# Grouped-query attention in a fused two-layer block: queries of two heads from seven of eight quarter products, with TensorE's order written out

## The chip, the cores and the metric

The kernel runs on one core of a Trainium2 chip. A core has a matrix engine (TensorE, "PE" in the profile, its weight loads "PEld"), a vector engine (VectorE, DVE), an activation engine (ScalarE, ACT), a general engine (GpSimd, POOL) and a synchronising engine (SyncE, SP). Each engine works off its own list of instructions in order; they meet through semaphores. Most DMAs are issued on SP's queue, those of the attention weights' turn on POOL's. The metric is the time of one execution on the device in microseconds (us); a kernel's time is the median of several runs.

## The reference

The whole computation is two blocks on x of shape 4 x 512 x 512 (batch rows b, 512 tokens, 512 channels): a gate, a Mamba-2 layer, a gate, a mixture of experts; then a gate, attention, a gate, an FFN. The change lies in the second block's attention, whose input x is already multiplied by its gate:

```python
b, sq, _ = x.shape                      # 4, 512, 512
q = jnp.einsum('bsh,he->bse', x, w_q).reshape(b, sq, GROUPS, HPG, KVC)   # 4 groups of 4 heads, 128
kv = jnp.einsum('bsh,he->bse', x, w_kv)
k, v = jnp.split(kv, 2, axis=-1)        # one key and one value head for each group
scores = jnp.einsum('bqgpd,bkgd->bgqpk', q, k) * (SCALE / LAYER_INDEX)
scores = jnp.where(causal[None, None, :, None, :], scores, -jnp.inf)
probs = jax.nn.softmax(scores, axis=-1)
ctx = jnp.einsum('bgqpk,bkgd->bqgpd', probs, v).reshape(b, sq, HEADS * KVC)
return jnp.einsum('bse,eh->bsh', ctx, w_dense)
```

All numbers are float32.

## The kernel before

Activations are kept transposed: a tile h of 128 x 4 x 512 holds, for one row b, 512 channels (four blocks k of 128 partitions) by 512 tokens. Attention runs over 64 heads in the order group g, row b, head i of the group; below, head n is 16g + 4b + i. The kernel is written with a framework that orders the instructions of each engine when the kernel is built, by their dependencies and the order of writing; `after(engine)` binds what is written inside it behind the last instruction written so far on that engine. The order is then fixed: a built program has one list for each engine.

Of a head's work there is:

- **queries** (L1648): four matmuls of 512 columns into pq, a PSUM tile of the tag "tp" (two buffers), and ACT's scaling into qT.
- **keys and values** (`start_group`, L1622), once for a group and row: four matmuls of 512 into pk, sixteen of 128 into pv, PSUM tag "mm" (four buffers), and two ACT copies.
- **scores** (L1663): for each of four blocks qi of 128 queries a matmul of (qi+1) x 128 columns into psc (tag "mm"); DVE adds the causal mask (L1677) and takes the negated maximum (L1679); ACT takes the exponential with its sum; DVE takes the reciprocal (L1685), scales (L1686) and turns 32 x 32 blocks (L1690) into `turned`, a tile with two copies. POOL then writes these to DRAM with four DMAs (L1698), and one more (`collect`, L1716) reads them back as pT, the transposed weights. Within `scores`, `nudge` lets one step of the gates of the coming layer be written on DVE and ACT (the lines 259 to 333).
- **context** (L1718): four matmuls of pT and v into pctx, PSUM tag "acc" (two buffers), and ACT's copy into cx, one of five buffers of the pool sm. It runs three heads behind the scores (`held`, `settle`). The last two heads are transposed by TensorE in place of the DMAs (ptp, L1729).
- **dense** (L1753), when a row's four contexts are there: sixteen matmuls of 512 into pd (tag "acc"), in four parts of four, after each of which DVE adds the part to the residual xr (L1765).

In the first group the same engines also combine the experts' results (pcb, L1521) and apply the gates that make h of rows 1 to 3 (`gated`, DVE L406). The pool gp has four buffers of the tag "h"; before, they hold the four rows' h through attention. A group's query weights (1 MB) and key and value weights come in one step ahead by `load_group` (L1487) into the pool wa, with two buffers.

The FFN after attention puts its weights ffg, ffu and ffd over the space of pools that attention used: the pool of the gates, cb (buffers rr of the experts' results), and wa. A load waits until whatever lay there is no longer read. The loads (L1886 to L1889) stand in a row on SP's queue.

Of the kernel before, what the change touches and what calls it, by code (L numbers as in the profile page):

```python
# [10 lines left out]
F32 = mybir.dt.float32  # L11
# [3 lines left out]
ALU = mybir.AluOpType  # L15
# [68 lines left out]
def block_kernel(ctx: ExitStack, tc: tile.TileContext, a: dict, out: bass.AP):  # L84
# [58 lines left out]
    def ps_mm(name):  # L143
        return ps.tile([P, 512], F32, tag="mm", name=name, bufs=4)
# [268 lines left out]
    def gated(l, b, xb, pool, part=slice(0, T), **kw):  # L413
        have((l, b))
        n = part.stop - part.start
        g = pool.tile([P, NC, n], F32, **kw)
        nc.sync.dma_start(out=g, in_=gts[l][b][:, :, part])
        apply_gate(g, xb[:, :, part])
        return g
# [1067 lines left out]
    def load_group(g):  # L1487

        wq = wa.tile([P, NC, HPG * KVC], F32, tag="wq", name="wq")
        w = HPG * KVC  # L1490
        nc.sync.dma_start(
            out=wq, in_=a["w_q"][:, g * w : (g + 1) * w].rearrange("(k p) m -> p k m", p=P)
        )
        wkv = wa.tile([P, 2, NC, KVC], F32, tag="wkv", name="wkv")
        for i in range(2):
            c0 = i * GROUPS * KVC + g * KVC
            nc.sync.dma_start(
                out=wkv[:, i], in_=a["w_kv"][:, c0 : c0 + KVC].rearrange("(k p) m -> p k m", p=P)
            )
        return wq, wkv  # L1500

# [37 lines left out]
    with tc.tile_pool(name="moe_w2", bufs=1, reuse_waits="tile") as wm:  # L1539
# [33 lines left out]
        n = len(nc.cur_bb.bb.instructions)  # L1573
        early_h = gated(2, 0, x[0], wa, tag="wq", name="h2_0")
        early_th = [
# [13 lines left out]
    with att as ph:  # L1589
# [25 lines left out]

        hs = [gp.tile([P, NC, T], F32, tag="h", name="h2")] + [None] * (B - 1)
        nc.sync.dma_start(out=hs[0], in_=early_h)

        class Group:
            pass  # L1620

        def start_group(g, b, w):  # L1622
            u = Group()
            u.g, u.b, u.ctxT = g, b, []
            u.last_row = g == GROUPS - 1 and b == B - 1
            u.wq, wkv = w
            u.h = h = early_h if (g, b) == (0, 0) else hs[b]
            pk = ps_mm("pk")
            for k in range(NC):
                nc.tensor.matmul(  # L1630
                    pk, lhsT=wkv[:, 0, k, :], rhs=h[:, k, :], start=(k == 0), stop=(k == NC - 1)
                )
            u.kT = sm.tile([P, T], F32, tag="kT", name="kT")
            nc.scalar.copy(u.kT, pk)
            pv = ps_mm("pv")
            for t in range(NT):
                for k in range(NC):
                    nc.tensor.matmul(  # L1638
                        pv[:, t * P : (t + 1) * P],
                        lhsT=h[:, k, t * P : (t + 1) * P],  # L1640
                        rhs=wkv[:, 1, k, :],
                        start=(k == 0),
                        stop=(k == NC - 1),
                    )
            u.v = sm.tile([P, NT, KVC], F32, tag="v", name="v")
            nc.scalar.copy(u.v.rearrange("p t d -> p (t d)"), pv)
            return u

        def queries(u, i):
            pq = ps_tp("pq")  # L1650
            for k in range(NC):
                nc.tensor.matmul(  # L1652
                    pq,
                    lhsT=u.wq[:, k, i * KVC : (i + 1) * KVC],
                    rhs=u.h[:, k, :],
                    start=(k == 0),
                    stop=(k == NC - 1),
                )
            qT = sm.tile([P, T], F32, tag="qT", name="qT")
            nc.scalar.mul(qT, pq, SCALE)  # L1660
            return qT

        def scores(u, i, qT):  # L1663
# [5 lines left out]
            for qi in range(NT):  # L1669
                n = (qi + 1) * P  # L1670
                if qi == 0:
                    collect(1)
                psc = ps_mm("psc")
                nc.tensor.matmul(  # L1674
                    psc[:, :n], lhsT=qT[:, qi * P : n], rhs=u.kT[:, :n], start=True, stop=True
                )
                nc.vector.tensor_tensor(psc[:, qi * P : n], psc[:, qi * P : n], mask, ALU.add)  # L1677
# [43 lines left out]
        def context(u, prs):  # L1721
# [18 lines left out]
            pctx = ps_acc("pctx")  # L1740
            for kj in range(NT):
                nc.tensor.matmul(  # L1742
                    pctx[:, kj * P :].rearrange("p (q r j) -> p q r j", r=QUAD, j=SQ),
                    lhsT=u.v[:, kj, :],
                    rhs=pT[:, :, 4 * kj : 10 + kj : 3, :].rearrange("p r q j -> p q r j"),
                    start=(kj == 0),
                    stop=(kj == NT - 1),
                )
            cx = sm.tile([P, T], F32, tag="cx", name="cx", bufs=5)
            nc.scalar.copy(cx, pctx)  # L1750
            u.ctxT.append(cx)

        def dense(u):  # L1753
            for m in range(NC):
                po = ps_acc("pd")
                for i in range(HPG):
                    nc.tensor.matmul(  # L1757
                        po,
                        lhsT=dense_w[u.g][:, i, m * P : (m + 1) * P],
                        rhs=u.ctxT[i],  # L1760
                        start=(i == 0),
                        stop=(i == HPG - 1),
                    )
                xs = x[u.b][:, m, :]
                nc.vector.tensor_tensor(xs, xs, po, ALU.add)  # L1765

        def settle():

            old, done = held.pop(0)
            context(old, done)
            if len(old.ctxT) == HPG:
                dense(old)

# [3 lines left out]
        def begin(n):  # L1779
            g, b, i = heads_[n]  # L1780
            if i == 0:
                if b == 0 and g + 1 < GROUPS:
                    weights[g + 1] = load_group(g + 1)
                groups[g, b] = start_group(g, b, weights[g])
            return groups[g, b], queries(groups[g, b], i)

# [8 lines left out]
        look_ahead(1, (0, 1))  # L1795
        groups = {}
        numbers = iter(range(GROUPS * B * HPG))
        ready, held = begin(0), []
        for n, (g, b, i) in enumerate(heads_):
# [8 lines left out]
            if g == 2 and i == 0 and b < 3:  # L1808
                to, name = ((ffg_d, "gateT"), (ffu_d, "upT"), (ffd_d, "downT"))[b]
                nc.sync.dma_start(out=to, in_=a[name])  # L1810
            if g and b == 0 and i == 3:
                dense_w[g] = load_dense(g)
            if n + 1 < len(heads_):
                ready = begin(n + 1)
            if g == 0 and i == 2 and b + 1 < B:
                act.use(act.EXP)
                hs[b + 1] = gated(2, b + 1, x[b + 1], gp, tag="h", name=f"h2_{b + 1}")
                act.use(act.LOG_EXP)
            prs = scores(u, i, qT)
            held.append((u, prs))  # L1820
            if len(held) > 3:
                settle()
            if n == len(heads_) - 2:
                last_row_over = [
                    i for i in nc.cur_bb.bb.instructions if i.engine == nc.scalar.engine
                ][-1]
        while held:
            settle()
        for _ in making:
            pass  # L1830
# [212 lines left out]
```

## Time and profile before

| | |
|---|---|
| median of three runs | 2239.01 us (2236.49 to 2239.73) |
| the profiled execution | 2242.7 us, span 2241.0 us, mean granted clock of TensorE 0.981 |
| attention, first group | 1120 to about 1334 us of the span |
| attention, second to fourth group | about 1334 to 1995 us |
| FFN | from 1973 (first matmuls, between attention's last) to the end |
| queries, TensorE busy (L1652) | 237.4 us, 512 records of 128x512 |
| dense, TensorE busy (L1757) | 222.4 us, 512 records of 128x512 |
| DVE waiting for dense (L1765) | 196.8 us |
| turned blocks: four DMAs a head (L1698), issue to landing | 208 KB each, 3.8 us |
| pT: one DMA a head (L1716), issue to landing | 832 KB, 7.3 us |

How to read the profile: a group of instructions is named by engine, line, output and input tile and shape; "busy" is the time in which the engine ran them. A matmul of float32 appears as two records. The durations of matmul records overlap and are modelled, so the true price of a row of matmuls is taken from the chain of waits, in which each piece begins where the one before ended. A window row gives, for a stretch of the span, its length and the busy time (and count) of PE, PEld, DVE, ACT and POOL, then the clock granted to TensorE (1.00 is full), the DMA engines' busy share, and GB/s. In the timeline a line is start, duration, engine, line, operation, output and input, shape, count, and in brackets how long the engine had been idle and what ended that.

### The profile page before, as it was taken

How to read it: one execution, taken by the hardware profiler on the slowest of the kernel's cores; microseconds unless marked ns; L12 is line 12 of the kernel's file. 1: busy time of each engine (PE TensorE's matmuls, PEld its weight loads, DVE VectorE, ACT ScalarE, POOL GpSimd, SP SyncE). 2: the span in 40 equal slices, each digit the busy share in tenths (PEclk: the TensorE clock that was granted, in tenths of full speed). 3: DMA queues.
4: the chain of work that ended last, by engine and by line, in shares of the span. 5: the costliest groups of instructions: out<-in, count | busy, mean ns of one | idle time of the engine just before them, and what ended most of it. 6: DMA issues, size and time to landing. Idle time of an engine off the chain costs nothing.

```text
span 2241.0 us, 23830 instructions
## 1 busy us (share of the span) xinstructions
PE 2135.2 (95%) x7570; PEld 1224.9 (55%) x7570; DVE 1526.2 (68%) x3039; ACT 968.9 (43%) x1899; POOL 455.8 (20%) x620
## 2 busy tenths in 40 slices
PE   4979999999999999999998999999999999999998
PEld 2545565565665444444454455555555555568887
DVE  8799889989653566676477766677767765555332
ACT  4576776765732234333254333333334432333221
POOL 4023242422222111222211111112112122100000
PEclk9989999999999999999989999999999999999999
DMA  7542341432424458988676555555645464531100
GB/s 257 195 132 73 107 155 67 156 122 67 167 83 141 152 190 285 382 289 285 211 252 195 179 183 150 160 164 181 185 140 175 141 195 140 185 122 38 38 20 20
DMA packets 112452, 357.38 MB, mean 159 GB/s; under 512 B 14592, under 2 KB 23168, under 8 KB 102912
## 3 DMA queue, kind: packets, MB, share of 16 engines
q1 hardware_dynamic: 78656, 224.43, 29.0%
q0 software_dynamic: 31360, 127.16, 18.9%
q10 hardware_dynamic: 2304, 4.20, 0.5%
q8 instruction: 62, 1.02, 0.2%
q14 instruction: 70, 0.57, 0.1%
HBM read 337.91 MB, written 108.00 MB: 199 GB/s over the span
## 4 chain that ended last, share of the span: by engine, by line
PE 40%; DVE 8%; ACT 1%; DMA 1%; issue 0%; DVEq 0%; ACTq 0%
PE pd L1757 10%; PE pq L1652 6%; PE pctx L1742 4%; PE psc L1674 4%; PE pk L1630 3%; PE pv L1638 3%; PE pfo L1873 2%; PE pfo L1872 2%; PE pfg L1872 2%; PE pfg L1873 2%; PE pfu L1872 2%; PE pfu L1873 2%; DVE nmax L1679 1%; DVE turned L1690 1%; DVE pr L1686 1%; DVE psc L1677 1%
## 5 line engine op out<-in xcount | busy, mean ns | idle before, releaser
L1698 POOL DMA_DIRECT2D turned<-turned x248 | 136.0, 555 | 622.8 <-DVE turned L1690 387.9
L128 ACT ACTIVATE pr<-psc,nmax 128x128 f32<-128x128 f32 (+3 forms) x256 | 134.7, 527 | 286.9 <-DVE nmax L1679 284.2
L1652 PE MATMUL pq<-h,wq 128*128 128x512 f32 x512 | 237.4, 599 | 1.8 <-DVE h L406 1.2
L1757 PE MATMUL pd<-cx,wd 128*128 128x512 f32 x512 | 222.4, 592 | 0.0
L1765 DVE TENSOR_TENSOR xr<-xr,pd 128x512 f32<-128x512 f32 x64 | 44.0, 687 | 196.8 <-PE pd L1757 196.8
L1674 PE MATMUL psc<-kT,qT 128*128 128x128 f32 (+3 forms) x512 | 160.0, 442 | 15.5 <-ACT pr L128 14.4
L1757 PEld LDWEIGHTS pd<-cx,wd 128*128 128x128 f32 x512 | 96.1, 190 | 114.8 <-issue 110.3
L1057 PE MATMUL pc<-h,wxb 128*128 128x512 f32 x320 | 145.6, 610 | 6.6 <-DVE h L406 4.0
L1652 PEld LDWEIGHTS pq<-h,wq 128*128 128x128 f32 x512 | 94.7, 193 | 102.2 <-issue 90.8
L1742 PE MATMUL pctx<-pT,v 128*128 128x512 f32 (+3 forms) x512 | 148.4, 433 | 0.0
L1742 PEld LDWEIGHTS pctx<-pT,v 128*128 128x128 f32 x512 | 96.7, 190 | 76.2 <-issue 50.5
L847 PE MATMUL po<-w,yT 128*128 128x512 f32 x296 | 134.2, 593 | 0.6 <-DMA w<-in_w2x 0.4
L814 PE MATMUL pg<-w,hT 128*128 128x512 f32 x296 | 134.2, 594 | 0.0
L825 PE MATMUL pn<-w,hT 128*128 128x512 f32 x296 | 133.4, 593 | 0.7 <-DMA w<-in_w1x 0.7
L1674 PEld LDWEIGHTS psc<-kT,qT 128*128 128x128 f32 x512 | 84.9, 191 | 74.2 <-ACT pr L128 29.7
L1679 DVE TENSOR_REDUCE nmax<-psc 128x1 f32<-128x128 f32 (+3 forms) x256 | 122.1, 481 | 2.1
L1690 DVE STREAM_TRANSPOSE turned<-pr 128x128 f32<-128x128 f32 x248 | 117.0, 493 | 1.2
L1128 PE MATMUL pz<-wzt,h 128*128 128x512 f32 x256 | 116.6, 605 | 0.3 <-ACT st L1229 0.3
L1276 PE MATMUL po<-wot,yT 128*128 128x512 f32 x256 | 115.4, 605 | 0.0
L1057 PEld LDWEIGHTS pc<-h,wxb 128*128 128x128 f32 x320 | 60.8, 195 | 78.0 <-issue 71.5
L1686 DVE TENSOR_SCALAR pr<-pr,rsum 128x128 f32<-128x128 f32 (+3 forms) x256 | 95.7, 375 | 2.2
L1677 DVE TENSOR_TENSOR psc<-psc,mask 128x128 f32<-128x128 f32 x256 | 70.9, 284 | 37.4 <-PE psc L1674 37.0
(348 smaller groups left out, 4186.3 us busy)
## 6 DMA issues: line engine op xcount, KB each, us to landing
w<-in_w1x SPq DMA_DIRECT2D x76, 1024.0 KB
turned<-turned POOLq DMA_DIRECT2D x248, 208.0 KB, 3.8
pT<-turned POOLq DMA_DIRECT2D x62, 832.0 KB, 7.3
w<-in_w2x SPq DMA_DIRECT2D x38, 1024.0 KB
wb<-in_b1x SPq DMA_DIRECT2D x38, 512.0 KB
lm<-cs SPq DMA_DIRECT2D x32, 512.0 KB
kt<-in_fT SPq DMA_DIRECT2D x62, 256.0 KB
ek<-ek SPq DMA_DIRECT2D x62, 256.0 KB
```

The lines of the kernel that those rows point to most:

```text
L128: nc.scalar.activation(*args, **kw)
L814: nc.tensor.matmul(pg, lhsT=hT[:, k, :], rhs=self.w1[s][0][:, k, :], start=(k == 0), stop=(k == NC - 1))
L1057: nc.tensor.matmul(pc, lhsT=wxb[:, k, m * P : (m + 1) * P], rhs=h[:, k, :], start=(k == 0), stop=(k == NC - 1),)
L1652: nc.tensor.matmul(pq, lhsT=u.wq[:, k, i * KVC : (i + 1) * KVC], rhs=u.h[:, k, :], start=(k == 0), stop=(k == NC - 1),)
L1674: nc.tensor.matmul(psc[:, :n], lhsT=qT[:, qi * P : n], rhs=u.kT[:, :n], start=True, stop=True)
L1679: nc.vector.tensor_reduce(nmax, psc[:, :n], AX.X, ALU.max, negate=True)
L1690: nc.vector.transpose(blocks[:, :, 3 * qi : 4 * qi + 1, :].rearrange("p c k j -> p k c j"), pr)
L1698: nc.gpsimd.dma_start(out=d[:, :, r].rearrange("c i s -> i c s"), in_=blocks[r * SQ : (r + 1) * SQ].rearrange("i c k j -> i c (k j)"),)
L1742: nc.tensor.matmul(pctx[:, kj * P :].rearrange("p (q r j) -> p q r j", r=QUAD, j=SQ), lhsT=u.v[:, kj, :], rhs=pT[:, :, 4 * kj : 10 + kj : ...
L1757: nc.tensor.matmul(po, lhsT=dense_w[u.g][:, i, m * P : (m + 1) * P], rhs=u.ctxT[i], start=(i == 0), stop=(i == HPG - 1),)
L1872: nc.tensor.matmul(out_, lhsT=w, rhs=xs[0], start=first_, stop=False)
L1873: nc.tensor.matmul(out_, lhsT=w, rhs=xs[1], start=False, stop=last_)
```

## The change

From the second group on, the queries of two neighbouring heads are made together. The weights of a pair, 512 channels by 2 x 128, are seen as four quarters (a11 and a12: first head, first and second half of the channels; a21 and a22: second head), and h as four quarters (halves of the channels by halves of the tokens). Seven products of quarters, each two matmuls of 256 columns, with sums of quarters as their operands, take the place of eight. The weights' sums s1 to s4 are made by POOL for each pair and group (`pair_weights`); the sums t1 to t4 of h by POOL in the first group (`mix`), once a row, and kept in DRAM beside h; from then on each row's h and ht (1 MB each) come back by two DMAs on SP's queue one row ahead (`load_row`), and share the four "h" buffers.

The products' results are put together by ACT (x1, y5), DVE (five adds from PSUM, `plus`) and POOL (two sums of y5), half a pair per head: `ahead(n)` makes p1, p6, p2, p7 in an even head and p5, p3, p4 in an odd one, two heads and one head before the pair's first head. Keys and values move there too, for the next row, behind heads 2 and 3 of a row. The binding `after(nc.tensor)` freezes TensorE's order in these groups. Dense is cut into its four parts, one after each of the next four heads (two after each of heads 2 and 3 of a group's first row). Its weights are loaded one row into the group. The contexts' copies cx use, four times in nine, the buffers rr of the pool cb. The first group works as before, with its weights in two pairs.

```diff
+    def pair_weights(g, j):
+        w = wa.tile([P, 2, NC, 2 * KVC], F32, tag=f"wq{1 - j}", name=f"wq{1 - j}", bufs=1)
+        load_pair(w[:, 0], g, j)
...
+        nc.gpsimd.tensor_tensor(s1, a21, a22, ALU.add)
+        nc.gpsimd.tensor_tensor(s3, a11, a21, ALU.subtract)
+        nc.gpsimd.tensor_tensor(s2, s1, a11, ALU.subtract)
+        nc.gpsimd.tensor_tensor(s4, a12, s2, ALU.subtract)
+        return a11, a12, a22, s1, s2, s3, s4
...
+        def mix(b, h):
+            ht = new_ht(b)
+            b11, b12, b21, b22 = quarters(h)
+            t1, t2, t3, t4 = (ht[:, i] for i in range(4))
+            nc.gpsimd.tensor_tensor(t1, b12, b11, ALU.subtract)
+            nc.gpsimd.tensor_tensor(t2, b22, t1, ALU.subtract)
+            nc.gpsimd.tensor_tensor(t3, b22, b12, ALU.subtract)
+            nc.gpsimd.tensor_tensor(t4, t2, b21, ALU.subtract)
+            nc.sync.dma_start(out=h_d[b], in_=h)
+            nc.sync.dma_start(out=t_d[b], in_=ht)
...
+        def in_turn(g):
+            return after(*[nc.tensor] * (g > 0))
...
+        def two_queries(u, j):
...
+            def plus(to, p, other, sign=1.0):
+                nc.vector.scalar_tensor_tensor(to, p, sign * SCALE, other, ALU.mult, ALU.add)
...
+            q0 = new_q(0)
+            with after(nc.tensor):
+                p1, p6 = two()
+                product(p1, a11, b11)
+                product(p6, s2, t2)
+            nc.scalar.mul(x1, p1, SCALE)
+            plus(u2, p6, x1)
+            with after(nc.tensor):
+                p2, p7 = two()
+                product(p2, a12, b21)
+                product(p7, s3, t3)
+            plus(q0[:, lo], p2, x1)
+            plus(u3, p7, u2)
+            yield q0
+            q1 = new_q(1)
+            with after(nc.tensor):
+                p5, p3 = two()
+                product(p5, s1, t1)
+                product(p3, s4, b22)
+            nc.scalar.mul(y5, p5, SCALE)
+            nc.gpsimd.tensor_tensor(u2, y5, u2, ALU.add)
+            nc.gpsimd.tensor_tensor(q1[:, hi], y5, u3, ALU.add)
+            plus(q0[:, hi], p3, u2)
+            with after(nc.tensor):
+                p4, _ = two()
+                product(p4, a22, t4)
+            plus(q1[:, lo], p4, u3, -1.0)
+            yield q1
...
-                nc.tensor.matmul(
-                    psc[:, :n], lhsT=qT[:, qi * P : n], rhs=u.kT[:, :n], start=True, stop=True
-                )
+                with in_turn(u.g):
+                    nc.tensor.matmul(
+                        psc[:, :n], lhsT=qT[:, qi * P : n], rhs=u.kT[:, :n], start=True, stop=True
+                    )
...
-            cx = sm.tile([P, T], F32, tag="cx", name="cx", bufs=5)
+            at = (u.b * HPG + len(u.ctxT)) % 9 if u.g else 0
+            if at < 5:
+                cx = sm.tile([P, T], F32, tag="cx", name="cx", bufs=5)
+            else:
+                cx = cb.tile([P, T], F32, tag=f"rr{at % 2}", name="cx", bufs=2)
...
+        def ahead(n):
+            if not g or n + 2 - i % 2 >= len(heads_):
+                return
+            s = n + 2 - i % 2
+            lead(s)
+            if i >= 2:
+                with after(nc.tensor):
+                    (keys_, values)[i - 2](groups[heads_[s][:2]])
...
             prs = scores(u, i, qT)
+            ahead(n)
             held.append((u, prs))
             if len(held) > 3:
                 settle()
+            dense_parts(1 if b or i < 2 else 2)
```

The scores of a head (L1793 in the changed kernel) stand on TensorE's list ahead of half a pair's products (L1741), then keys or values, context (L1862), and the part of dense (L1882).

## The prediction

> **What bounds the kernel now.** I read the page's busy shares first, then the windows of attention, one for each row of a group, then the chain of waits inside them.
>
> ```profile
> span 2241.0 us, 23830 instructions
> ...
> PE 2135.2 (95%) x7570; PEld 1224.9 (55%) x7570; DVE 1526.2 (68%) x3039; ACT 968.9 (43%) x1899; POOL 455.8 (20%) x620
> ```
>
> ```profile
> 1388.00:1440.00 52.00, 52.00 (x171) 28.16 (x171) 35.22 (x98) 20.23 (x50) 10.99 (x20) 1.00 0.62 183
> 1440.00:1495.00 55.00, 54.49 (x177) 29.35 (x176) 41.00 (x108) 20.21 (x51) 11.06 (x20) 1.00 0.54 164
> ...
> 1598.00:1649.00 51.00, 51.00 (x165) 27.47 (x165) 32.85 (x89) 20.05 (x47) 10.98 (x20) 1.00 0.61 182
> ```
>
> The second number of each row is the window, the third PE's busy time: from the second group on PE has no gap, at full clock. DVE works 33 to 41 us of some 52, POOL 11. So a microsecond of PE work removed there is a microsecond won, and each new wait of PE is a microsecond lost. The chain gives PE's true prices, since its pieces follow end on start:
>
> ```profile
> 1388.21 13.73 PE pd L1757 x32
> 1401.95 2.16 PE psc L1674 x8
> 1404.10 2.16 PE pctx L1742 x8
> 1406.26 3.44 PE pq L1652 x8
> ...
> 1589.14 3.57 PE pv L1638 x32
> ```
>
> Each matmul is two records: 0.430 us a record of 512 columns (pq), 0.112 of 128 (pv). A line through both has 0.0055 us for a record and 0.00083 for a column; it gives 2.17 for the four score matmuls (measured 2.16), and 0.218 for a record of 256 columns.
>
> **What is won.** A pair of heads now takes 2 x 3.44 = 6.88 us of queries. Seven products of two matmuls of 256 columns are 28 records: 28 x 0.218 = 6.10. That is 0.78 a pair, 24 pairs (three groups, four rows, two pairs): **-18.8 us**. If a record cost only its columns it would be 20.6; 15 if a 256-column record's fixed part were twice as large.
>
> **What waits instead.** Number the heads n = 16g + 4b + i. In the changed program's order of instructions PE's order is frozen: scores of n (four matmuls, L1793), half a pair's products, context, one quarter of dense (four matmuls), scores of n+1. The third score matmul needs the upper half of qT. For the first head of a pair that half is written by DVE (the add of p3), which needs POOL's sum u2 + y5, and POOL has that sum behind the four transfers of the turned blocks. In DVE's queue this add stands, for ten heads (22, 26, 30, 34, 38, 42, 48, 54, 58, 62), behind the masks, maxima, reciprocals, scalings and mostly the transposes of the same head's first two score tiles. DVE cannot start those before PE's first two score matmuls, and PE cannot go past the third until they are over. This is a loop in the order, not a matter of load. (Head 18 has it too, but there PE has a context and six dense matmuls, 7.3 us, in between.) Its price, from start to start of DVE's instructions in the timeline of one head before:
>
> ```profile
> 1567.45 0.30 DVE L1677 TENSOR_TENSOR psc<-psc,mask 128x128 f32<-128x128 f32 x1 [2.28 <-PE psc L1674]
> 1567.78 0.29 DVE L1679 TENSOR_REDUCE nmax<-psc 128x1 f32<-128x128 f32 x1
> ...
> 1568.60 0.16 DVE L1685 RECIPROCAL rsum<-rsum 128x1 f32<-128x1 f32 x1
> ...
> 1568.87 0.28 DVE L1686 TENSOR_SCALAR pr<-pr,rsum 128x128 f32<-128x128 f32 x1
> ...
> 1569.39 0.30 DVE L1690 STREAM_TRANSPOSE turned<-pr 128x128 f32<-128x128 f32 x1
> ...
> 1575.57 0.46 DVE L1677 TENSOR_TENSOR psc<-psc,mask 128x128 f32<-128x128 f32 x2
> ```
>
> Put t = 0 where PE ends the dense quarter of the head before. DVE's residual add takes it to 0.7 (row xr<-xr,pd, 687 ns, next start 0.1 sooner); masks at 0.7 and 0.9, maxima at 1.1 and 1.3; from the maximum to the reciprocal 0.82 (1567.78 to 1568.60: ACT's exponential is inside); scaling 2.1, transpose 2.4, the second tile's reciprocal, scaling and transpose 2.6, 2.8 and 3.15; the add at 3.5. No row has an add of 128x256 from PSUM: between the 128x128 mask (285 ns) and the 128x512 residual add (687) it is 420. So 3.9, and PE goes on at about 4.1, with 0.65 us of matmuls done: a stall of 3.45 us (head 58; 3.0 at 62, which has no transposes). Each gate step between adds 0.6 (elementwise) to 1.15 (scan) less what hides behind the exponential: 3.8 at heads 26, 30 and 48 (one step), 4.8 at 42 (two), 5.5 at 34 (three). Seven heads: **+28**. Floor, 2.4 each if masks and maxima are ready at once: +17; ceiling, POOL's sum later by 1 us each: +36.
>
> Heads 22, 38 and 54 come after two heads without a dense quarter (the first row of a group, i = 0 and 1). There PE's work is 7.8 (scores 2.16, eight product matmuls 3.48, context 2.16) and 6.9 us. DVE's softmax of one head is 8.12 (1567.45 to 1575.57) less three gate steps of 0.6, so 6.3; with adds (1.1, then 0.4) and three steps (0.85 a mean one) 10.0 and 9.3. The scores' four PSUM buffers let PE lead by no more than a head, so 2.2 + 2.4 is lost, and the loop's 2.7 at head 22: 7.3; with one step more 8.5 at 38; 3.4 at 54, where no gates are left. With 1 for POOL: **+20**, from 8 (DVE catches up) to 26.
>
> **The clock after a stall.** Before, in the first group, PE slows after a wait:
>
> ```profile
> 1152.46 1.62 PE L1674 MATMUL psc<-kT,qT 128*128 128x128 f32 x6
> 1155.98 1.67 PE L1674 MATMUL psc<-kT,qT 128*128 128x512 f32 x2 [1.90 <-ACT pr L128]
> ...
> 1184.03 2.07 PE L1674 MATMUL psc<-kT,qT 128*128 128x512 f32 x2 [5.84 <-ACT pr L128]
> 1185.90 4.22 PE L1652 MATMUL pq<-h,wq 128*128 128x512 f32 x8
> ```
>
> Two 512-column records show 1.02 at full clock (1148.17), four pairs of a head's queries 3.60: here 2.07 and 4.22, 1.7 us lost behind 5.84 of idling; and 1.67 behind a mere 1.90. Seven stalls of 3 to 5.5 us at 1.7, and 2 for the heads where DVE is the limit anyway: **+14**, from 0 to 28 (2.8 lost at the first keys of attention, 6.44 against 3.60, ten times). [...]
>
> **The FFN's weights.** The context of a head now goes, four times in nine, into the buffers rr of the pool cb, and the last row's third and fourth are among them. In the built program the first load of ffu waits for the last dense matmul that reads one of these, and all other loads stand behind it on SP's queue. Before, they were issued long ahead:
>
> ```profile
> 1945.84 0.70 SPq L1886 DMA_DIRECT2D ffg<-ffg_d  x1
> ...
> 1961.48 7.09 SPq L1889 DMA_DIRECT2D ffd<-ffd_d  x3
> ```
>
> First used at 1973.51, with dense over at 1995. Now they start there: the first cut, eight of 192 KB, is 1.6 MB, at 378 to 402 GB/s (windows 1945 to 1975) 4 us and about 2 to land; the next eight of 512 KB take 11 more, so 17, against 11 us of matmuls in the first cut. PE loses 6 at the start, 1 at the second cut, 1 to the clock: **+8**, from 4 (only the first landing) to 16 (half the rate). The frozen order also takes away the FFN matmuls that filled the last two heads' transposes: **+2**.
>
> **Costed at nothing, with cover.** ACT: two scalings of 512 (594 ns) become two of 256; it is 20 us of 52. POOL: two sums a pair at about 0.65 (y<-y,zs is 1426 ns mean for 512 columns) and 24 weight sums, 72 x 0.65 = 47 us over twelve rows, in each of which POOL is busy 11 of 52; behind them wait the turned blocks, wanted a head later. The four sums for each row of the first group (1.2 to 1.4 each) stand before the turned blocks where PE idles some 20 us: +1 (-2 to +10). [...] SP: 2 MB a row more on a queue with DMA at 0.5 to 0.6, issued two heads ahead, some 22 us: covered; if not, products wait for ht.
>
> **Sum.** -18.8 + 28 + 20 + 14 + 8 + 2 + 1 = +54. The profiled execution took 2242.7 (span 2241.0), 3.7 over the median 2239.01; so 2297 as profiled, 2293 as median.
>
> **Rivals.** A: the stalls are there but short: DVE's spacing at its floor (+17), catching up in the first rows (+8), no clock loss, weights +4, so +11: 2250. For it: DVE is idle a quarter of its time. Against: the 1.90 us gap. 17%, taken as all of 2240 to 2260. B, the other side: the added waits fall into time that DVE has ready, below 1.7 us for each of the eleven places (18.8/11), the point from which the matmul gain decides. It needs the third score matmul to be released without the two softmax tiles before it; with only gate-free, half-second waits and FFN weights early, 2239 - 18.8 + 11 x 0.5 = 2226. For it: PE at 100% rewards each product left out. Against: DVE's queue as built. 4%. C: DVE, with ten adds of 0.42 a row busy 37 to 45 us of 50, becomes the bound in every row of the first two rounds, or ht comes late: eight rows by 5 us more, 2333. 5%. That the gain itself is missing, 28 records at 0.245: +0.78 x 24 = 2312, inside the range. Forecast: 74%.
>
> **Range.** The forecast's own is 2260 to 2322 (half-way or so from 54 to the sum of the floors, -18.8 + 17 + 8 + 0 + 4 = +10, and to that of the ceilings, over +90). To leave out at most a fifth (10 of A's 17%, B, C) it reaches into A: 2252 to 2322. A measurement here can tell 0.2% (4.5 us) from nothing: faster 4%, same 2% (A's lower edge), slower 94%.
>
> **What would show it.** Right: 672 product records near 0.218 spacing; at the ten heads an idle PE of 3 to 6 us at L1793 put down to DVE; granted clock below 1.00 in the windows of attention; the first ffu load after the last dense, and PE waiting for a DMA at the first pfg. Wrong: gaps at the ten heads under 1.7, or at other heads; FFN weights landing before dense ends.

## The result, and the profile after

The changed kernel takes 2325.97 us (median of six runs, 2314.15 to 2329.51) against 2239.37 for the kernel before (six runs, 2234.99 to 2244.34): 1.0379 times as long, 95% interval 1.0352 to 1.0407. The direction is that of the prediction; the time lies 33 us above it and 4 above its range. The page of the changed kernel:

```profile
span 2327.7 us, 24789 instructions
...
PE 2154.0 (93%) x7858; PEld 1300.7 (56%) x7858; DVE 1586.5 (68%) x3160; ACT 960.8 (41%) x1898; POOL 534.0 (23%) x708
```

PE does less work and is busy 19 us longer: part of its work runs at a lower clock. The windows of attention, two rows of some 58 to 60 us and one of 51 (window, PE busy, PE's weight loads, DVE, ACT, POOL, granted clock, DMA share, GB/s):

```profile
1584.00:1642.00 58.00, 51.71 (x193) 33.15 (x192) 39.55 (x104) 20.03 (x49) 14.73 (x24) 0.94 0.57 178
1643.00:1703.00 60.00, 52.86 (x193) 34.03 (x192) 39.16 (x107) 19.30 (x48) 13.75 (x24) 0.91 0.59 193
1761.00:1812.00 51.00, 50.43 (x194) 32.73 (x193) 35.91 (x92) 17.25 (x44) 18.33 (x28) 1.00 0.61 189
```

In a slow row PE stands 6 to 7 us and its clock is 0.91 to 0.94; in the fast one neither. PE's waits from 1340 to 2080 (sum, times, longest):

```profile
PE psc L1793 <- DVE qT L1748: 48.1, 11, 7.1
PE pctx L1862 <- DMA pT<-turned: 10.7, 2, 9.1
PE pfu L2047 <- DMA ffu<-ffu_d: 2.1, 1, 2.1
```

One of the eleven is at each of heads 22, 26, 30, 34, 38, 42, 48, 54, 58 and 62, the ten that the prediction named, and a short one (0.57) at head 46. The ten come to 47.5 us; nine are of 3.3 to 7.1, the one at head 62 is of 0.6. Head 30, in the timelines of PE, DVE and POOL (start, duration; in brackets the idle time before and what ended it):

```profile
1566.84 3.60 PE L1882 MATMUL pd<-cx,wd 128*128 128x512 f32 x8
1570.27 0.82 PE L1793 MATMUL psc<-kT,qT 128*128 128x128 f32 x4
1577.41 3.32 PE L1793 MATMUL psc<-kT,qT 128*128 128x384 f32 x4 [6.32 <-DVE qT L1748]
```

```profile
1571.63 0.71 DVE L1809 STREAM_TRANSPOSE turned<-pr 128x512 f32<-128x512 f32 x1
1572.27 0.65 DVE L1890 TENSOR_TENSOR xr<-xr,pd 128x512 f32<-128x512 f32 x1
1572.84 0.49 DVE L1796 TENSOR_TENSOR psc<-psc,mask 128x128 f32<-128x128 f32 x2
...
1575.12 1.29 DVE L1805 TENSOR_SCALAR pr<-pr,rsum 128x128 f32<-128x128 f32 x2
1576.34 0.62 DVE L1809 STREAM_TRANSPOSE turned<-pr 128x128 f32<-128x128 f32 x2
1576.89 0.38 DVE L1748 SCALAR_TENSOR_TENSOR qT<-pq,u 128x256 f32<-128x256 f32 x1
```

```profile
1572.64 2.19 POOL L1817 DMA_DIRECT2D turned<-turned  x4 [8.28 <-DVE turned L1809]
1574.84 0.73 POOL L1772 TENSOR_TENSOR u<-x,u 128x256 f32<-128x256 f32 x1
```

PE is through with its first two score matmuls at 1571. DVE still transposes the last tile of head 29, then takes head 30's first two tiles as far as their transposes, and only then makes the add at 1576.89. POOL's sum, which the add needs, cannot be earlier than 1574.84 either: it stands behind four issues, and these wait for the transpose at 1571.63. At 1577.41 four records that take 1.58 us at full pace take 3.12 to the next start.

Where the 86.7 us between the two profiled executions went, by the starts of PE's pieces: 7.4 before the first keys of attention, where PE has the same instructions in both programs (over the profiles below that point lies anywhere from 1110 to 1128 us); 10.2 in the first group (203.1 to 213.3); 63.4 from the second group to the last dense matmul (671.9 to 735.3); 5.6 from there to the end (245.9 to 251.5).

### The profile page after: what moved, and what is told of

It reads as the page before. It is cut to its first block, busy times and chain, and to the rows that moved or that the text cites. A ratio compares the mean times of both kernels' runs of the same rounds, so it can differ in the third digit from the quotient of the medians.

```text
span 2327.7 us, 24789 instructions
## 1 busy us (share of the span) xinstructions
PE 2154.0 (93%) x7858; PEld 1300.7 (56%) x7858; DVE 1586.5 (68%) x3160; ACT 960.8 (41%) x1898; POOL 534.0 (23%) x708
## 4 chain that ended last, share of the span: by engine, by line
PE 39%; DVE 9%; DMA 2%; POOL 1%; issue 1%; ACT 1%; POOLq 0%; DVEq 0%; SPq 0%; ACTq 0%
PE pd L1882 9%; PE pq L1741 5%; PE pctx L1862 5%; PE psc L1793 4%; PE pv L1702 2%; PE pk L1691 2%; PE pfo L2048 2%; PE pfo L2047 2%; PE pfu L2047 2%; PE pfg L2047 2%; PE pfg L2048 2%; PE pfu L2048 2%; DVE turned L1809 1%; DVE nmax L1798 1%; DVE pr L1805 1%; PE pq L1718 1%
## 5 line engine op out<-in xcount | busy, mean ns | idle before, releaser
L1882 PE MATMUL pd<-cx,wd 128*128 128x512 f32 x512 | 227.4, 593 | 0.0
L1793 PE MATMUL psc<-kT,qT 128*128 128x128 f32 (+3 forms) x512 | 170.2, 469 | 58.8 <-DVE qT L1748 48.1
L1862 PE MATMUL pctx<-pT,v 128*128 128x512 f32 (+3 forms) x512 | 153.8, 444 | 11.4 <-DMA pT<-turned 10.7
L1793 PEld LDWEIGHTS psc<-kT,qT 128*128 128x128 f32 x512 | 88.5, 199 | 113.1 <-issue 66.5
L1882 PEld LDWEIGHTS pd<-cx,wd 128*128 128x128 f32 x512 | 94.2, 191 | 102.1 <-issue 100.2
L1862 PEld LDWEIGHTS pctx<-pT,v 128*128 128x128 f32 x512 | 98.3, 195 | 78.6 <-issue 52.6
L1809 DVE STREAM_TRANSPOSE turned<-pr 128x128 f32<-128x128 f32 x248 | 122.0, 499 | 1.3
L1805 DVE TENSOR_SCALAR pr<-pr,rsum 128x128 f32<-128x128 f32 (+3 forms) x256 | 100.6, 396 | 1.2
L1741 PE MATMUL pq<-ht,wq 128*128 128x256 f32 x384 | 99.8, 383 | 0.0
L1171 ACT ACTIVATE lm<-lm,cs 128x128 f32<-128x128 f32 x256 | 81.7, 390 | 23.6 <-DMA lm<-cs 23.6
L1072 DVE SCALAR_TENSOR_TENSOR xc<-pc,cols,xc 128x509 f32<-128x509 f32 (+2 forms) x120 | 84.5, 736 | 8.6 <-ACT xc L1068 8.5
```

Of the source, the lines that this page charges most:

```text
L1741: nc.tensor.matmul(out_, lhsT=w[:, c], rhs=xs[:, c], start=(c == 0), stop=(c == 1))
L1793: nc.tensor.matmul(psc[:, :n], lhsT=qT[:, qi * P : n], rhs=u.kT[:, :n], start=True, stop=True)
L1809: nc.vector.transpose(blocks[:, :, 3 * qi : 4 * qi + 1, :].rearrange("p c k j -> p k c j"), pr)
L1862: nc.tensor.matmul(pctx[:, kj * P :].rearrange("p (q r j) -> p q r j", r=QUAD, j=SQ), lhsT=u.v[:, kj, :], rhs=pT[:, :, 4 * kj : 10 + kj : ...
L1882: nc.tensor.matmul(po, lhsT=dense_w[u.g][:, i, m * P : (m + 1) * P], rhs=u.ctxT[i], start=(i == 0), stop=(i == HPG - 1),)
```

## The experiments

Every run is timed beside the kernel before; ratios are to that. Single profiles differ by up to 18 us in what precedes attention, so the reading goes by stretches: "group one" is from the first keys to the keys of the second group, "groups two to four" from there to the last dense matmul.

**1. freed.** The score matmuls no longer wait for the late add.

```
-            plus(u3, p7, u2)
+            plus(q0[:, hi], p7, u2)
...
-            nc.gpsimd.tensor_tensor(q1[:, hi], y5, u3, ALU.add)
-            plus(q0[:, hi], p3, u2)
+            nc.gpsimd.tensor_tensor(q1[:, hi], y5, u2, ALU.add)
+            plus(u3, p3, u2)
```

> Same instructions, operands rewired: the upper half of the first head's queries is written by the add of p7, a head earlier, and the add of p3 goes to scratch (so the queries of three groups are other sums than the reference's). If the loop (third score matmul behind its own head's softmax in DVE's queue) is the cause, the ten waits of 3.3 to 7.1 us at L1793 (48 us in all) go, and the clock that is lost behind them (about 2 us each) with them: 2326 - 48 - 20 = 2258, granted clock 1.00 from head 20 on. If DVE or POOL as a whole is what holds PE in the second and third group, the idle time turns up at other lines and the time stays above 2300. If the low clock has another cause than the waits, about 2278 with the clock still at 0.8 to 0.9 somewhere in each row.

Measured: 2339.48 us, 1.0443 (1.0401 to 1.0485), slower and not faster. The waits at the scores are gone, and longer ones stand at the next products (waits of PE, then POOL, DVE and PE at head 30; a ninth wait, of 10.8, is at the same place of head 34, and the list gives no releaser for it):

```profile
PE pq L1741 <- DVE u L1748: 57.8, 8, 9.4
```

```profile
1567.80 0.74 POOL L1772 TENSOR_TENSOR u<-x,u 128x256 f32<-128x256 f32 x1
```

```profile
1575.32 0.39 DVE L1748 SCALAR_TENSOR_TENSOR u<-pq,u 128x256 f32<-128x256 f32 x1
```

```profile
1575.76 2.08 PE L1741 MATMUL pq<-h,wq 128*128 128x256 f32 x4 [9.40 <-DVE u L1748]
```

The same add also reads p3 out of the PSUM buffer that the next p1 and p6 are written to, and here it comes after all four tiles of the head's softmax. So the third score matmul was only the first of two doors that the late add keeps shut. What matters is why it is late. Here it does not wait for POOL: the sum is over at 1568.54, and DVE, never idle, comes to the add 6.8 us later, because DVE's list has it behind the softmax.

**2. whole.** Queries of a head in one product again (four matmuls of 512 columns), in the same frozen order, with the same loads, spills and spread dense product.

```
-        nc.gpsimd.tensor_tensor(s1, a21, a22, ALU.add)
...
-        return a11, a12, a22, s1, s2, s3, s4
+        return w
...
+            for i in range(2):
+                q = new_q(i)
...
+                nc.scalar.mul(q, pq, SCALE)
+                yield q
```

> Only the quarter products undone: each head's queries are one product again, in the same frozen order, two heads ahead, with the same loads, spills and spread dense product; no weight sums and none of the five adds of a pair. Theory: no wait at L1793 above 1 us, PE loses the 20 us of matmuls that the quarters save: 2326 - 68 + 20 = 2278; the wait of the context for pT (9.2 us at head 18) stays if loads cause it, and goes (another -12) if POOL's sums cause it. If the frozen order or the spread dense product is what stalls PE, waits of 3 us and more remain in every row and the time stays above 2310.

Measured: 2263.17, 1.0098 (1.0065 to 1.0132), lower than expected by 15, since the wait for pT went as well. A window over ten rows:

```profile
1400.00:1950.00 550.00, 550.00 (x1795) 300.01 (x1795) 367.62 (x999) 202.50 (x501) 117.30 (x215) 1.00 0.63 196
```

PE never stands. In these ten rows the frozen order, the spread dense product and 2 MB of loads a row cost nothing by themselves; nine of the eleven rows take 51.7. Groups two to four as a whole take 677.2, 5.3 more than before: in the last row the dense product waits 4.7 us for cx, and the clock falls behind it (its next sixteen records take 9.14 us from 1977.41, at full pace 6.88). Group one (212.2) and the end (251.2) keep their loss.

**3. thaw.** The changed kernel with the freeze taken out of scores, products, contexts and dense.

```
-            return after(*[nc.tensor] * (g > 0))
+            return after()
...
-            with after(nc.tensor):
+            with after():
```

> The changed kernel with PE's order left to the planner in all groups (products, scores, contexts, dense), everything else as changed, POOL's sums too. If the freeze is what makes the loop costly, PE has dense or products to do while DVE reaches the add of p3, the ten waits shrink to under 2 us each and the time falls to 2326 - 50 = 2275 or less. If the add behind the softmax is costly in any order, waits of 3 us and more remain and the time stays above 2300.

Measured: 2334.60, 1.0419 (1.0390 to 1.0449). Its longest waits are others:

```profile
PE pctx L1862 <- DMA pT<-turned: 39.7, 12, 8.2
PE psc L1793 <- DVE qT L1748: 20.5, 17, 2.6
```

The waits for DVE's adds shrink, as the first theory had it, to 2.6 or less at the scores (at the products there are four more, 10.5 in all and 3.6 at most), and the context waits instead for pT, which POOL loads. So PE's frozen order alone is not the cause either.

**4. u2_dve and both_dve.** The sum on which the add waits is made by DVE; in the second run the other sum, q1's, too, behind the add of p3.

```
-            nc.gpsimd.tensor_tensor(u2, y5, u2, ALU.add)
+            nc.vector.tensor_tensor(u2, y5, u2, ALU.add)
```

> One instruction of a pair moved: the sum u2 + y5, which POOL makes behind the four transfers of the turned blocks, is made by DVE; the built order then has the add of p3 ahead of the next head's masks and maxima, while the other sum stays on POOL. The run before showed that freeing the scores alone moves the wait to the next products, whose PSUM bank the same add must first read. If POOL's place in this chain is what puts the add behind the softmax, both waits go: ten waits (48 us) and some 20 us of clock, 2326 - 68 = 2258, with the 9 to 11 us for pT at heads 17 and 18 still there. If DVE is the limit by itself, the waits stay above 3 us each and the time above 2310.

> Both sums of a pair on DVE, none on POOL. As the run beside it, and POOL no longer stands 16 us on the second sum at the start of group two (1353.7 to 1369.7 in the changed kernel) with the load of pT behind it: if that is why the context waits for pT (1.5 and 9.2 us, and 2.5 of clock), these go too: 2258 - 13 = 2245. If the loads of h and ht (2 MB at the same time) make pT late, the wait stays and the time is that of the run beside it, plus up to 5 for 24 more sums on DVE.

Measured: 2264.89, 1.0113 (1.0091 to 1.0135), and 2260.88, 1.0103 (1.0084 to 1.0122). One instruction a pair moved wins some 60 us. The waits of the first, and DVE at head 26:

```profile
PE psc L1793 <- DVE qT L1748: 11.0, 4, 4.8
PE pctx L1862 <- DMA pT<-turned: 4.9, 2, 3.1
```

```profile
1494.20 0.40 DVE L1772 TENSOR_TENSOR u<-x,u 128x256 f32<-128x256 f32 x1
1494.59 0.40 DVE L1748 SCALAR_TENSOR_TENSOR qT<-pq,u 128x256 f32<-128x256 f32 x1
1495.30 0.41 DVE L1748 SCALAR_TENSOR_TENSOR qT<-pq,u 128x256 f32<-128x256 f32 x1
...
1496.83 0.49 DVE L1796 TENSOR_TENSOR psc<-psc,mask 128x128 f32<-128x128 f32 x2
```

With the sum on DVE the built order has the adds ahead of the next head's masks. So the hinge is that this sum stands on POOL, behind the turned blocks. Two things go with that, a late sum and a late place of the add on DVE's list, and no run parts them: none has the sum on POOL and the add early. At head 30 of the changed kernel the list alone costs little (the sum is over at 1575.57, the add starts at 1576.89), in freed it costs all of the 6.8 us. Against expectation the first run already cuts the wait for pT to 4.9, and the second only to 4.2 (one of 3.0 at another row): so the sum still on POOL was not what kept it. In place of the long wait for pT, PE waits at head 18 for queries, 4.8 and 3.7 us.

**5. cx.** The last row's contexts stay out of the rr buffers.

```
-            at = (u.b * HPG + len(u.ctxT)) % 9 if u.g else 0
+            at = (u.b * HPG + len(u.ctxT)) % 9 if u.g and not u.last_row else 0
```

> The contexts of the last row use only the five cx buffers, none of the rr buffers. If the late FFN weights are the price at the end, the first load of ffu is issued before the last dense product, PE's 2.1 us wait at the first pfu and the slow start go, and the stretch from the last dense matmul to the end falls from 252 to 246 us: 2320. If the loads are bound by rate or by another buffer, the stretch stays at 252 and the time at 2326.

Measured: 2314.29, 1.0323 (1.0288 to 1.0359). From the last dense matmul to the end 245.1 us, where the changed kernel has 251.5; the first FFN product starts 22 us before the last dense one is over. This term is settled: 6.4 us. (The rest of the 12 lies ahead of attention.)

**6. spill and mix_late.** The two spills of a row from POOL's queue; then the sums and spills a head later.

```
-            nc.sync.dma_start(out=h_d[b], in_=h)
-            nc.sync.dma_start(out=t_d[b], in_=ht)
+            nc.gpsimd.dma_start(out=h_d[b], in_=h)
+            nc.gpsimd.dma_start(out=t_d[b], in_=ht)
```

```
-        mix(0, hs[0, 0][0])
...
-                mix(b + 1, h)
...
+            if n == 0:
+                mix(0, fresh)
+            if g == 0 and i == 3 and b + 1 < B:
+                mix(b + 1, fresh)
```

> The two spills of each row (h_d, t_d) are issued from POOL's queue in place of SP's. In the changed kernel SP issues t_d at 1143.39, when POOL's sums are done, and the three loads of rr behind it at 1143.80; PE waits 6.70 us for them at 1149.83. If SP's queue is what the first group lost, the stretch from the first keys of group one to the first keys of group two falls from 213 us to 203-206, and the time by 7 to 10, to about 2317. If POOL's sums (25 us more) or the 8 MB of spills themselves cost it, the stretch stays at 210 or above and the time does not change, or rises as POOL's turned blocks are issued later.

> The changed kernel with the four sums and two spills of each row of group one later: the first row's behind the scores of head 0 (so behind the first loads of rr in SP's queue), the others' a head later, behind that head's turned blocks. If the place in the queues costs the first group its 10 us, the stretch from first keys to the keys of group two falls from 212 to 216 us (four runs so far) to 203 to 206, and the time to about 2317. If the 8 MB of spills, the 25 us of sums or the buffers of h cost it wherever they stand, it stays at 210 or more.

The reason for spill stands in SP's queue and PE's timeline of the changed kernel:

```profile
1143.39 0.32 SPq L1661 DMA_DIRECT2D t_d<-ht  x1
1143.80 2.44 SPq L1529 DMA_DIRECT2D rr<-rows_o  x3
```

```profile
1149.83 1.11 PE L1542 MATMUL pcb<-ident,rr 128*128 128x128 f32 x4 [6.70 <-DVE rr L1537]
```

Measured: spill 2323.43, 1.0362 (1.0319 to 1.0406), mix_late 2313.44, 1.0324 (1.0307 to 1.0341). With the spills off SP the wait for rr falls from 6.70 to 0.20, and group one is still 216.2: the scores wait for their PSUM buffers instead (22.7 us in all, 9.5 in the changed kernel). With the work later it is 210.3. Neither comes down to 203 to 206: the queue is a real wait, but not what the group lost.

**7. all, no_sums and sums_dve.** all has both sums on DVE, mix_late and cx together; no_sums and sums_dve start from it.

```
             t1, t2, t3, t4 = (ht[:, i] for i in range(4))
-            nc.gpsimd.tensor_tensor(t1, b12, b11, ALU.subtract)
+            nc.vector.tensor_tensor(t1, b12, b11, ALU.subtract)
...
```

> Both sums on DVE, the mixing late and the last row's contexts out of rr, together: 2326 - 68 (waits and clock) - 13 (pT) - 8 (first group) - 6 (FFN weights) = 2231, with all of the 20 us of matmuls saved kept: 10 under the kernel before. If the first group keeps its cost, 2239, no difference that can be measured; if DVE becomes the bound with 48 sums more, above 2250.

> The run all, with POOL's sixteen sums of group one left out: the quarters of h themselves are spilled in their place (four transfers of the same bytes), so the products of the later groups are of other inputs than the reference's. In group one of the changed kernel DVE is busy 167 us, before 152; the gating at L406 takes 1084 ns a time, before 682, L276 1203 against 682, L328 1767 against 1253. If POOL's sums lengthen DVE's instructions, these fall back to 682 and 1253 and the stretch of group one from 211 to 203-206, the time to about 2248. If the spills or the queue cost it, the durations may fall but the stretch stays at 209 or above.

> The run all, with the sixteen sums of group one made by DVE. If interference is the cost, L406 and L328 fall back to 682 and 1253 ns, saving some 10 us of DVE, against 16 sums at 0.68 = 11: DVE is busy as long as before, and the stretch stays at 209 to 212, the time at 2255 within 3. If POOL's lateness (not DVE's time) is the cost, the stretch falls to 205.

Measured: all 2254.81, 1.0077 (1.0047 to 1.0106); no_sums 2249.83, 1.0045 (1.0028 to 1.0063); sums_dve 2247.85, 1.0031 (1.0007 to 1.0055). Group one: 211.0, 206.6 and 210.0, before 203.1. DVE's gating of h in group one, in the kernel before and the changed one (busy, mean ns):

```profile
L406 DVE SCALAR_TENSOR_TENSOR h<-th,h 128x512 f32<-128x512 f32 x15 | 9.7, 682 | 0.4 <-DVEq L1579 0.3
```

```profile
L406 DVE SCALAR_TENSOR_TENSOR h<-th,h 128x512 f32<-128x512 f32 x15 | 15.7, 1084 | 0.7 <-ACT th L128 0.3 <-DVEq L1600 0.3
```

In all, the sums meet another instruction (DVE, then POOL):

```profile
1246.19 4.05 DVE L1805 TENSOR_SCALAR pr<-pr,rsum 128x128 f32<-128x128 f32 x1
```

```profile
1246.43 1.28 POOL L1656 TENSOR_TENSOR ht<-h 128x512 f32<-128x512 f32 x1
1247.68 1.26 POOL L1658 TENSOR_TENSOR ht<-h 128x512 f32<-128x512 f32 x1
1248.90 1.25 POOL L1657 TENSOR_TENSOR ht<-h,ht 128x512 f32<-128x512 f32 x1
```

A scaling that takes 0.28 us in the kernel before takes 4.05 here and ends at 1250.24, with POOL's third sum (1250.15). Without the sums, and with them on DVE, the same scaling takes 291 and 284 ns in the mean (828 in all) and the gating 680: that POOL's sums hold up DVE is shown. How much of group one that is, is less sharp, since one profile does not tell 3 us there. The profiles with the sums as changed show 212.2 to 216.6 (eight runs), with the sums on POOL but later 210.0 to 211.0 (mix_late, all, tail), with the sums on DVE 210.0, 204.4 and 206.2 (sums_dve and the two below, whose first group is the same), without them 206.6, and before 203.1.

**8. tail, stage and stage_cx.** tail is all with PE's order open in the last row; stage is sums_dve with p1, p6, p5, p3 after an even head's scores, p2 and p7 after its dense quarter and p4 alone after the odd head's; stage_cx adds the copy of the last contexts on DVE.

```
-                p2, p7 = two()
+                p5, p3 = two()
...
+            plus(q0[:, hi], p3, u2)
+            nc.vector.tensor_tensor(q0[:, hi], y5, q0[:, hi], ALU.add)
+            yield None
+            with after(nc.tensor):
+                p2, p7 = two()
...
-            nc.scalar.copy(cx, pctx)
+            (nc.vector.tensor_copy if u.last_row else nc.scalar.copy)(cx, pctx)
```

> The run all, with PE's order left open from the last row on (scores of its last two heads, its contexts and dense product). FFN products can then fill the 4.7 us wait of dense for cx at 1967.7, its clock (1.6) and the waits of the last transposes: 2255 - 6 = 2249; the forecast's term for it was 2. If the order built without the freeze is no better, 2255.

> The run sums_dve, with the products of a pair in another order: p1, p6, p5, p3 after the scores of the even head, p2 and p7 after its dense quarter, p4 alone after the odd head's scores, so that both halves of the first head's queries are written a whole head before they are read; the second head's as late as before. If the waits left at L1793 (10.0 us at four heads, 1.1 to 4.8 each) are the same add coming late in DVE's queue, they go, and some 3 us of clock with them: 2248 - 13 = 2235. If DVE is behind with the softmax itself at those heads, the wait turns up at another line and the time stays within 4 of 2248.

> The run beside it, and the contexts of the last row are copied by DVE instead of ACT. In sums_dve dense waits 4.6 us (and 1.5 to 3 us of clock) for the copy at 1967.19, which stands in ACT's queue behind the exponentials and casts of the FFN's inputs. If that queue is the cause, 6 us go: 2229, and the kernel is faster than the one before (2239) by 0.4%: the 20 us of matmuls less the 7 us of the first group and 3 us of pT. If it is given back later, 2235.

Measured: tail 2252.88, 1.0057 (1.0037 to 1.0076), no difference from all that these intervals show, the wait of dense for cx still 4.4. stage 2245.18, 1.0033 (1.0012 to 1.0054); stage_cx 2244.53, 1.0018 (1.0002 to 1.0033). The waits of stage:

```profile
PE pctx L1863 <- DMA pT<-turned: 6.1, 2, 5.3
PE pd L1883 <- ACT cx L1875: 5.7, 2, 4.6
PE psc L1794 <- ACT pr L128: 4.9, 5, 2.0
```

The late add is gone from the list, and at three of its four heads PE now waits for the exponential (that is, for DVE's maxima before it): DVE is behind with the softmax there, which was the rival. On DVE, the copy of cx is waited for just as long (4.8). That does not clear ACT's queue, since in DVE's the copy stands behind the other half of the same work, the gating and splitting of the FFN's inputs, though its context was made at 1958.9 (DVE in stage_cx):

```profile
1961.45 2.08 DVE L406 SCALAR_TENSOR_TENSOR h<-th,h 128x512 f32<-128x512 f32 x3 [1.25 <-ACT th L128]
...
1964.65 1.89 DVE L2040 TENSOR_TENSOR h_lo<-h,h_hi 128x512 fp32r<-128x512 f32 x3
1966.46 0.69 DVE L1875 COPY cx<-pctx 128x512 f32<-128x512 f32 x1
```

A copy ahead of that work was not tried. No version beats the kernel before. The gain itself is real: seven of stage's eleven rows take 50.1 to 50.6 us, nine of whole's 51.7. It is spent in the other four (60.9, 53.0, 57.4 and 52.6), where PE's waits lie.

## Why the prediction came out short

**The gain.** Forecast 18.8 with 0.218 us a record. Four records in the changed kernel:

```profile
1380.18 1.03 PE L1741 MATMUL pq<-h,wq 128*128 128x256 f32 x4
1381.04 1.03 PE L1741 MATMUL pq<-ht,wq 128*128 128x256 f32 x4
```

0.865 from start to start, 0.216 a record: 6.88 - 28 x 0.216 = 0.83 a pair, 20 in all. Right.

**The waits.** Forecast 28 + 20 = 48, measured 47.5 at the ten heads named. Single heads miss both ways: 4.7, 6.3, 6.3, 5.5, 3.8, 3.4 and 0.6 at the seven (30.6 against 28), 6.5, 7.1 and 3.3 at the three (16.9 against 20). At head 30 (6.3 against 3.8) DVE came to the residual add 2 us late, and two scalings took 1.29 beside POOL's sums. The reason given was half of it: "a loop in the order" is right for the first door, but runs 1 and 3 show that opening it, or freeing PE's order, moves the wait elsewhere, and run 4 that the place of the add on DVE's list comes of the sum on POOL. The near agreement of the total owes something to luck.

**The clock.** Forecast 14 (seven stalls of 1.7, and 2). Nine loop stalls of 3.3 to 7.1 us cost 1.7 to 3.0 each, 19.6 in all, and the wait for pT 2.2: the term was mis-sized, with nine places where it priced seven, and 2.2 a place where it had 1.7. At head 22, for instance, four score records and sixteen product records take 6.92 from 1461.41, at full pace 1.58 + 3.46. The row with 1.90 us, by which the prediction had short waits slow the clock as well, did not hold: after a wait of the same 1.90 in the changed kernel the same two records show 1.12, not 1.67. In all and sums_dve, waits of 1.1, 1.8 and 2.3 cost nothing, those from 3.0 on 1.5 to 3.1; one of 2.1 in u2_dve is followed by 1.7 lost. There are exceptions: in thaw a wait of 2.65 cost nothing, and eight product records right after one of 3.3 ran at full pace; in both_dve the keys of the second group took 5.2 after a wait of 1.4 (with two of 0.5 and 0.7 just before it), in u2_dve 3.5 after the same waits. In freed and stage the same keys took 5.2 as well, and after a wait of 2.3 the four score records, which take 1.58 in all and sums_dve, took 3.1 in no_sums and tail. So no sharp bound comes out of these runs.

**What failed: the turned blocks, "costed at nothing, with cover", and the first group, "+1 (-2 to +10)".** The prediction counted POOL's busy time (47 us over twelve rows), took the turned blocks as "wanted a head later", and gave waits for pT no term. At head 18 it even took the context that PE's list has ahead of the third score matmul as cover, 7.3 us with six dense matmuls. That context has to wait (POOL, then PE):

```profile
1390.52 0.56 POOL L1835 DMA_DIRECT2D pT<-turned  x1
```

```profile
1402.06 4.61 PE L1862 MATMUL pctx<-pT,v 128*128 128x512 f32 x8 [9.15 <-DMA pT<-turned]
1406.46 5.68 PE L1882 MATMUL pd<-cx,wd 128*128 128x512 f32 x12
1411.98 1.67 PE L1793 MATMUL psc<-kT,qT 128*128 128x384 f32 x4
```

The load lands 11.4 us after its issue. The same load takes as long in whole (10.9) and u2_dve (11.3), and PE does not wait for it there, because products and the next row's keys stand ahead of this context on PE's list. In spill, with all the sums on POOL, the long wait is absent as well. So the 9.15 us come of where the built order put the context; why it put it there is not shown. They do not come of POOL standing, which is the other thing to be seen at this place:

```profile
1369.74 0.73 POOL L1772 TENSOR_TENSOR u<-x,u 128x256 f32<-128x256 f32 x1 [16.00 <-ACT x L1771]
...
1373.84 0.56 POOL L1835 DMA_DIRECT2D pT<-turned  x1
```

POOL stands 16 us on a sum whose product PE makes after the dense product of the row before, with a load of pT behind it; but that load ends the shorter wait, 1.5 us at head 16. In u2_dve POOL stands 17.9 us there on the other sum, and PE waits 1.8. The two waits and the clock behind the long one are 12.9 us in all; whole has neither.

The second thing left out is that POOL's sums hold up DVE: part of the 10.2 of the first group, forecast as +1. In the changed kernel the gating takes 1084 ns a time, without the sums 680; in all a scaling of 0.28 becomes 4.05 beside three sums in a row (run 7).

**The end.** FFN forecast 8, measured 5.6 (run 5 takes 6.4 back). Of the "about 2 to land" in it: SP issues the first load of ffu at 2076.34, and PE's wait for it ends at 2078.74, 2.4 later. The two last heads' transposes wait 3.3 us in all (forecast 2).

The sum after the fact, in the order of the prediction: -20 + 48.1 + 19.6 (clock of the loop) + 5.6 (FFN) + 10.2 (first group) + 12.9 (pT) + 2.8 (what is left of the 63.4, the transposes among it) + 7.4 (ahead of attention) = 86.6, measured 86.7. Of the 33 us missing, 22 are the wait for pT and the first group, 6 the clock's and 7 that one execution's start; the gain and the FFN give 3 or so back.

## What to carry to other kernels

Before splitting an operation into parts that three engines add up, follow each intermediate sum to its queue: not how long it takes, but what the instruction ahead of it there waits for, and what then stands behind. A sum of 0.7 us, once a pair, on the engine that also issues transfers cost some 60 us here over 24 pairs. Before counting a matmul as cover for a wait, look when its own input lands. When an experiment removes one wait, look whether the same late instruction keeps a second door shut, such as the PSUM buffer it still has to read.

## What the runs showed of the hardware

In the run all, a DVE scaling in SBUF that took 0.28 us in the kernel before took 4.05 beside three POOL sums in SBUF of 1.25 to 1.28 in a row, and ended within 0.1 us of the third; the mean of such scalings in the first group was 828 ns there, and 291 and 284 without the sums and with them on DVE. From the second group on, in the changed kernel, all and sums_dve, waits of PE up to 2.3 us mostly left its clock alone, and those of 3.0 and more cost 1.5 to 3.1 us of matmul time, with little dependence on their length (9.15 us cost 2.2). Other runs have exceptions on both sides: after 1.4 us both_dve, freed and stage lost 1.7, after 2.1 to 2.3 u2_dve, no_sums and tail 1.5 to 1.7; after 3.3 thaw lost nothing in eight product records.
